# Constant tables copied by ScalarE, batch norm in three chunks, deeper fetch in the second convolution, and another order table for the main stage

## The chip, the cores and the metric

The kernel runs on one core of one Trainium2 chip. The metric is device microseconds (us) from the start to the end of one execution. The core has TensorE (PE in the profile), VectorE (DVE), ScalarE (ACT), GpSimd (POOL) and SyncE (SP). Each works off its own list of instructions in order; an instruction that must wait for another engine waits on a semaphore, and what stands behind it in the same list waits too. In this kernel all DMA transfers are issued by SP.

## The reference, cut to what matters

Input x is 128 images of 128 channels and 16 by 16 places, f32. Two layers are applied.

```
# layer 0
h   = act_quant(bn(groupnorm(x)))                 # 4-bit activations
out = conv3x3(h, weight_quant(w1) * pat1)         # 5 of 9 taps
out = conv3x3(act_quant(bn(out)), weight_quant(w2) * pat2) + groupnorm(x)
x   = x + out
# layer 1, on tokens t = x as [128, 256, 128]
t = t + mamba(ln(t), fwd) + reversed(mamba(ln(reversed t), bwd))
      # in_proj; causal conv of 4 taps; silu; dt = softplus(.); A = -exp(A_log)
      # chunks of 64: exp(segsum(dt*A)) * (C B^T) applied to x*dt, plus carried states
      # y * silu(z), RMS norm, out_proj
t = t + moe(ln(t))        # router over 8 experts, softmax, top 2, expert matrices
```

## The kernel before, in words

**Stages.** The program is one long function, `tile_conv_attn_hybrid_kernel`. (1) A setup stage builds constants, loads x in 64 tiles `xr[i]` of two images each (128 channels by 512 values, 256 KB), quantises the first convolution's weights and computes group norm and batch norm statistics. (2) `conv1` runs over 64 pairs of images: quantise (L525, L527, L192), 5 matmuls (L218), statistics (L542). (3) `conv2` does the second convolution over the same 64 pairs, reads back the first's output from DRAM for all but the first 8 pairs (`fetch`, L615), transposes the result to tokens (L631) and stores it. (4) The main stage runs layer 1 over the 64 pairs. The first three stages are ordered by a scheduler; the main stage stands exactly in the order in which a loop at its end calls its parts.

**Setup.** Two constant tables, `rows0` and `cols0`, hold patterns for later matmuls. POOL fills them in `patterns()` (L376) from `heads` and `triple`, which POOL makes with 18 select instructions (L101, L105). They are stored to DRAM by two DMAs (L489, L490), which stand in SP's list behind the loads of x (L371), the 53 small weight loads of `load_weights` (L278 to L307) and the load of the second convolution's weights (L401). Group norm statistics are taken in four chunks of 48, 48, 24 and 8 images (`cuts`, L414). Per chunk: DVE takes `bn_stats` of each image, except every fourth one, which ACT sums with two passes (L441, L457); DVE combines them in small steps on 128xn tiles (L453 to L468); PE averages over groups with the matrix `grp` (L472, L478); ACT takes a square root (L481); `normed` (L420 to L434) makes a reciprocal with one Newton step and the scales. After the fourth chunk DVE forms the batch norm's scale `sc1` and shift `bi1` (L495 to L511), which every first step of `conv1` needs. The tiles of `conv1` are allocated in memory that the setup stage's tiles leave.

**Main stage.** Each pair goes through parts, each a generator whose steps are placed one by one: `a` layer norm and transposes, `c` time steps and decay (once for two pairs), `x` and `z` projections with the 4-tap convolution on DVE (L895), `xt`, `g`, `s`, `b`, `m` the chunk matrices, `y` their product with x, then gating on POOL (L1028) and squares on ACT; `n` adds the squares on POOL (L1037); `r` sums them on PE (L1045), transposes and takes a power on POOL (L1060); `o` is the output projection (L1072, L1082); `e` the second layer norm and the router, 31 steps, of which 13 in a row are small DVE steps that each read the one before (L1122 to L1145), one power on POOL (L1147), and more small steps; `p` multiplies the tokens by each expert's gate on POOL (L1177); `f` the expert matmuls (L1189). PSUM banks are few: two for x, z and s, two for y and f, four for the rest.

**Order.** `T` (L1200) gives each step a place; a period of 375 places covers two pairs, and the even and the odd pair have places of their own. L1276 adds 375 for each further two pairs, sorts all steps and calls them in that order. So at any place of the list, parts of about ten different pairs are interleaved.

**Keep apart.** Two small helpers bind DVE and POOL: `alone` (L575) remembers the latest small DVE instruction, and `large` (L578) makes the next large POOL instruction (L1028, L1037, L1177) wait for it. Which DVE step a POOL product waits for thus follows from the order in `T`.

Of the kernel before, what the change touches and what calls it, by code (L numbers as in the profile page):

```python
# [14 lines left out]
P = 128  # L15
NT = 256
# [18 lines left out]
def kernel(ctx: ExitStack, tc: tile.TileContext, a: dict):  # L35
# [60 lines left out]
    nc.gpsimd.memset(heads, 0.0)  # L96
    nc.gpsimd.memset(triple, 0.0)
    for m in range(2):
        for q in range(3):
            for t in (3 + 4 * q, 15 + 4 * q):  # L100
                nc.gpsimd.affine_select(  # L101
                    out=heads, in_=heads, pattern=[[-1, NH]], compare_op=ALU.not_equal,
                    fill=-1.0, base=-(64 + 32 * m + t), channel_multiplier=1,
                )
            nc.gpsimd.affine_select(  # L105
                out=triple[:, m : m + 1], in_=triple[:, m : m + 1], pattern=[[0, 1]], compare_op=ALU.not_equal,
                fill=1.0, base=-(64 + 32 * m + q), channel_multiplier=1,
            )
# [114 lines left out]
    def by_weights(how, phase, taps):  # L223

        some = nc.values_load(how[0:1, 0:1], min_val=0, max_val=2)
        with tc.If(some > 0) as cmp:
            with tc.If(some > 1) as cmp2:
                phase(range(9), 3)
            with cmp2.Else():
                phase(range(9), 1)  # L230
        with cmp.Else():
            phase(taps, 1)
# [111 lines left out]
    with tc.tile_pool(name="w1p", bufs=1) as w1p:  # L344

        grp = w1p.tile([P, P], F32, name="grp")
        nc.gpsimd.affine_select(
            out=grp, in_=ones, pattern=[[-4, 32], [0, 4]], compare_op=ALU.is_ge, fill=0.0,
            base=0, channel_multiplier=1,
        )  # L350
        nc.gpsimd.affine_select(
            out=grp, in_=grp, pattern=[[4, 32], [0, 4]], compare_op=ALU.is_ge, fill=0.0,
            base=3, channel_multiplier=-1,
        )
        nc.vector.tensor_scalar(grp, grp, 0.25, None, ALU.mult)
# [4 lines left out]
        with tc.tile_pool(name="setup1", bufs=1) as setup, tc.tile_pool(  # L360
            name="psa", bufs=1, space=PSUM
        ) as psa:
            w1 = w1p.tile([P, 9, P], F32, name="w1", tag="w")
            nc.sync.dma_start(w1, a["L0_conv_w1"])
            weights = conv_weights(wq1, how1, w1p, psa, w1, pat1, CROSS, "c1")
            for _ in range(3):
                next(weights)


            for i in range(NP):  # L370
                nc.sync.dma_start(xr[i], x_c[:, 2 * i : 2 * i + 2, :])  # L371
            rows0 = setup.tile([P, NH, 2, 2, P], BF16, name="rows0")
            cols0 = setup.tile([P, 2, 2, 2, 2, P], BF16, name="cols0")
            far = setup.tile([HD, 1], BF16, name="far")

            def patterns():  # L376
                nc.gpsimd.memset(far, -1e30)
                for h in range(NH):
                    nc.gpsimd.tensor_copy(
                        rows0[:, h].rearrange("p d t l -> p (d t l)"), heads[:, h : h + 1].to_broadcast([P, 4 * P])  # L380
                    )
                    nc.gpsimd.tensor_copy(
                        rows0[0:HD, h].rearrange("p d t (f l) -> p (d t f) l", l=HD),
                        ident[0:HD, 0:HD].unsqueeze(1).to_broadcast([HD, 2 * 2 * 2, HD]),
                    )
                for m in range(2):
                    for d in range(2):
                        sign = 1 - 2 * d
                        nc.gpsimd.tensor_copy(
                            cols0[:, m, d].rearrange("p j f l -> p (j f l)"), triple[:, m : m + 1].to_broadcast([P, 4 * P])  # L390
                        )
                        for half in range(2):
                            nc.gpsimd.affine_select(
                                out=cols0[0:HD, m, d, :, half, :], in_=far.unsqueeze(2).to_broadcast([HD, 2, P]),
                                pattern=[[0, 2], [sign, P]], compare_op=ALU.is_ge, fill=0.0,
                                base=-sign * HD * half - 1, channel_multiplier=-sign,
                            )

            load_weights()
            w2 = w1p.tile([P, 9, P], F32, name="w2", tag="w")  # L400
            nc.sync.dma_start(w2, a["L0_conv_w2"])  # L401

# [11 lines left out]
            cuts = [0, 3 * B // 8, 3 * B // 4, B - max(B // 16, 1), B]  # L414

            def by_scalar(b):

                return b % 4 == 3 and b < cuts[3]

            def normed(c):  # L420

                of = slice(cuts[c], cuts[c + 1])
                var_, gm_, dev_, ga_, qv_, dm_ = (t[:, of] for t in (var, gm, dev, ga, qv, dm))
                nc.vector.reciprocal(ga_, ga_)
                nc.vector.tensor_tensor(dm_, ga_, ga_, ALU.mult)
                nc.vector.tensor_tensor(dm_, dm_, qv_, ALU.mult)
                nc.vector.tensor_scalar(dm_, dm_, -0.5, 1.5, ALU.mult, ALU.add)
                nc.vector.tensor_tensor(ga_, ga_, dm_, ALU.mult)
                nc.vector.scalar_tensor_tensor(shift[:, of], gm_, -1.0, ga_, ALU.mult, ALU.mult)
                nc.gpsimd.tensor_scalar(ares[:, of], ga_, 1.0, SCALE, ALU.add, ALU.mult)  # L430
                nc.gpsimd.tensor_scalar(bres[:, of], shift[:, of], SCALE, None, ALU.mult)
                nc.vector.tensor_tensor(dev_, dev_, ga_, ALU.mult)
                nc.vector.tensor_tensor(var_, var_, ga_, ALU.mult)
                nc.vector.tensor_tensor(var_, var_, ga_, ALU.mult)  # L434

            for c in range(4):
                of = slice(cuts[c], cuts[c + 1])
                for b in range(B)[of]:
                    x_b = xr[b // 2][:, b % 2, :]
                    if by_scalar(b):  # L440
                        nc.scalar.activation(junk, x_b, AF.Copy, accum_out=bst[:, b, 1:2])  # L441
                    else:
                        behind = nc.vector.bn_stats(bst[:, b, :], x_b)
                if c > 0:

                    with tc.issue_after(behind.ins):
# [3 lines left out]
                if mine:  # L450

                    picked = slice(mine[0], cuts[c + 1], 4)
                    nc.vector.tensor_scalar(neg[:, picked], bst[:, picked, 1], -1.0 / NT, None, ALU.mult)  # L453
                    nc.vector.tensor_scalar(bst[:, picked, 1], neg[:, picked], -1.0, None, ALU.mult)
                    nc.vector.tensor_scalar(bst[:, picked, 4], neg[:, picked], -1.0, None, ALU.mult)
# [6 lines left out]
                nc.vector.tensor_tensor(mean_, bst[:, of, 1], bst[:, of, 4], ALU.add)  # L462
                nc.vector.tensor_scalar(mean_, mean_, 0.5, None, ALU.mult)
                nc.vector.tensor_tensor(dm_, bst[:, of, 1], bst[:, of, 4], ALU.subtract)
                nc.vector.tensor_tensor(dm_, dm_, dm_, ALU.mult)
                nc.vector.tensor_tensor(var_, bst[:, of, 2], bst[:, of, 5], ALU.add)
                nc.vector.tensor_scalar(dm_, dm_, 0.25, None, ALU.mult)
                nc.vector.scalar_tensor_tensor(var_, var_, 1.0 / NT, dm_, ALU.mult, ALU.add)  # L468
# [4 lines left out]
                nc.vector.tensor_copy(gm_, gm_ps)  # L473
                nc.vector.tensor_tensor(dev_, mean_, gm_, ALU.subtract)
                nc.vector.tensor_tensor(qv_, dev_, dev_, ALU.mult)
                nc.vector.tensor_tensor(qv_, qv_, var_, ALU.add)
# [3 lines left out]
                nc.vector.tensor_scalar(qv_, gv_ps, EPS, None, ALU.add)  # L480
                nc.scalar.activation(ga_, qv_, AF.Sqrt)  # L481
# [3 lines left out]
                if c == 1:  # L485
                    for _ in weights:
                        pass
                    patterns()
                    nc.sync.dma_start(rows_d, rows0)  # L489
                    nc.sync.dma_start(cols_d, cols0)  # L490
                if c == 3:
# [79 lines left out]
        by_weights(how1, conv1, CROSS)  # L571
# [33 lines left out]
    def conv2(taps, nq):  # L605
        with tc.tile_pool(name="pc", bufs=6) as pc, tc.tile_pool(
# [8 lines left out]
            def fetch(i):  # L615
                if NP > i and i not in kept:
                    qs[i] = pc.tile([P, 2, NT], F32, name=f"q2_{i}", tag="q")
# [31 lines left out]
            for i in range(5):  # L649
# [3 lines left out]
            for i in range(NP):  # L653
                b = 2 * i
                fetch(i + 5)
# [24 lines left out]
    by_weights(how2, conv2, DIAGONAL)  # L680
# [499 lines left out]
    def part_f(i):  # L1180
# [7 lines left out]
        for e in range(NE):  # L1188
# [10 lines left out]
    PERIOD = 375  # L1199
    T = {  # L1200
        ('a',): [[60, 68, 103, 165, 270, 336], [191, 257, 313, 327, 385, 395]],
        ('c',): [
            [420, 423, 452, 460, 468, 479, 483, 502, 515, 520, 522, 523, 526, 534, 537, 543, 548, 549, 581,
             602, 627, 630, 658, 669, 672, 676, 719, 727, 747, 823, 824, 862, 936],
        ],
        ('x', 0, 0): [[598, 604, 609, 613, 622], [783, 784, 790, 791, 805]],
        ('x', 0, 2): [[624, 631, 638, 640, 644], [809, 816, 830, 833, 834]],
        ('x', 0, 1): [[657, 662, 673, 689, 691], [849, 857, 867, 873, 875]],
        ('x', 1, 2): [[681, 684, 701, 703, 712], [866, 879, 881, 891, 896]],
        ('x', 1, 0): [[704, 705, 728, 733, 734], [894, 902, 922, 925, 927]],  # L1210
# [101 lines left out]
```

## Time and profile before

| | |
|---|---|
| runs, median (lowest to highest) | 2554.55 us (2553.18 to 2557.51) |
| the profiled execution's own time | 2554.94 us |
| its span, first to last instruction | 2553.1 us |
| setup, to the first quantising step of conv1 | 0 to 85.7 us |
| conv1 | 85.7 to 173 us |
| conv2 | 173 to 292.3 us |
| main stage, to the first pair's result (L1192 at 438.0) | 292.3 to 438 us |
| main stage, the rest | 438 to 2553.1 us |

Busy shares over the span: PE 95%, DVE 88%, ACT 85%, POOL 64%. The span stands 1.8 us below its execution's time, and that execution 0.4 us above the median. An idle engine costs nothing unless another waits for it; a wait shows as idle time in front of an instruction with the name of what ended it.

### The profile page before, as it was taken

Reading aid. Unit: us, or ns where it says so; the run is one execution under the profiler, and the core shown is the slowest. Engines: PE = TensorE matmul, PEld = TensorE weight load, DVE = VectorE, ACT = ScalarE, POOL = GpSimd, SP = SyncE. Lnnn points to the kernel's source line nnn. Section 1 sums busy time; section 2 is a strip of 40 time slices with the busy share of each in tenths; the row PEclk is TensorE's granted clock in tenths of the full one; section 3 lists DMA queues with packets and bytes.
Section 4 is the critical chain, followed back from the end, with each engine's and each line's share of the span. In section 5 each row is a group of like instructions: output and inputs, shape, how many; then the busy total and the mean of one; then the engine's idle time right before and its main releaser. Section 6 shows DMA issues by size and latency. Waiting matters only on the chain.

```text
span 2553.1 us, 49290 instructions
## 1 busy us (share of the span) xinstructions
PE 2415.3 (95%) x15940; PEld 1479.9 (58%) x15940; DVE 2253.2 (88%) x6163; ACT 2173.0 (85%) x4455; POOL 1629.3 (64%) x1694
## 2 busy tenths in 40 slices
PE   0688889999999999999999999999999999999997
PEld 0235456666666666666666666666666666666663
DVE  8787699999999999999999999999999999999883
ACT  5678699888889998889898888998988899898881
POOL 3468026676666666666666666666667666666666
PEclk9999899999999999999999999999999999999998
DMA  9358633434444444444444344444433443443343
GB/s 287 124 192 281 227 67 110 125 111 123 130 124 122 122 125 118 120 132 128 120 126 124 114 119 129 128 121 119 129 118 117 132 132 121 123 123 116 107 125 107
DMA packets 302167, 339.58 MB, mean 133 GB/s; under 512 B 56768, under 2 KB 226752, under 8 KB 301888
## 3 DMA queue, kind: packets, MB, share of 16 engines
q1 hardware_dynamic: 301888, 336.21, 43.3%
q8 instruction: 133, 2.18, 0.3%
q14 instruction: 146, 1.20, 0.2%
HBM read 262.72 MB, written 56.62 MB: 125 GB/s over the span
## 4 chain that ended last, share of the span: by engine, by line
PE 88%; DMA 4%; DVE 3%; ACT 2%; issue 1%; SPq 1%; POOL 1%; POOLq 0%; ACTq 0%; DVEq 0%
PE f_ps L1189 17%; PE x_ps L877 13%; PE y_ps L1012 10%; PE z_ps L920 9%; PE o_ps L1072 9%; PE sg L965 5%; PE xt_ps L932 4%; PE y_ps L1018 4%; PE g_ps L951 4%; PE cv L218 4%; DMA xr<-in_x 2%; PE n_ps L1045 1%; PE u_ps L1094 1%; PE f_ps L1184 1%; PE u_ps L750 1%
## 5 line engine op out<-in xcount | busy, mean ns | idle before, releaser
L1177 POOL TENSOR_TENSOR gb<-gb,u2T 128x512 f32<-128x512 f32 x512 | 641.3, 1277 | 122.7 <-PE y_ps L1018 68.8
L895 DVE SCALAR_TENSOR_TENSOR xc<-x_ps,cw,xc 128x510 f32<-128x510 f32 (+2 forms) x768 | 571.7, 744 | 46.5 <-ACT xc L889 36.9
L1028 POOL TENSOR_TENSOR yg<-yg,z 128x512 f32<-128x512 f32 x256 | 325.9, 1279 | 352.1 <-DVE yg L1024 155.1
L1189 PE MATMUL f_ps<-gb,ew 128*128 128x512 f32 x1024 | 510.1, 602 | 6.7 <-POOL gb L1177 6.4
L877 PE MATMUL x_ps<-uT,wx 128*128 128x512 f32 x768 | 402.9, 607 | 7.6 <-ACT e L731 3.3
L731 ACT ACTIVATE e<-sg 128x512 f32<-128x512 f32 x512 | 299.3, 591 | 49.9 <-PE sg L965 44.4
L731 ACT ACTIVATE e<-e,ends 128x128 f32<-128x128 f32 x1024 | 325.0, 392 | 0.0
L1012 PE MATMUL y_ps<-e,xt 128*64 128x256 f32 x2048 | 317.8, 389 | 0.2 <-DVE yg L1024 0.2
L993 DVE TENSOR_TENSOR e<-e,g_ps 128x1024 f32<-128x1024 f32 x256 | 311.6, 1217 | 5.5 <-ACT e L731 2.4
L895 DVE SCALAR_TENSOR_TENSOR bc<-x_ps,cw,bc 128x510 f32<-128x510 f32 (+2 forms) x384 | 286.7, 747 | 20.5 <-ACT bc L889 4.1
L1189 PEld LDWEIGHTS f_ps<-gb,ew 128*128 128x128 f32 x1024 | 180.5, 192 | 174.2 <-issue 136.2
L920 PE MATMUL z_ps<-uT,wz 128*128 128x512 f32 x512 | 271.2, 611 | 1.5 <-ACT xc L889 1.0
L889 ACT ACTIVATE xc<-x_ps,cb,cw 128x512 f32<-128x512 f32 x256 | 199.0, 777 | 64.0 <-PE x_ps L877 57.4
L1072 PE MATMUL o_ps<-wo,yg 128*128 128x128 f32 x2048 | 251.4, 276 | 0.2 <-DVE e L998 0.2
L1072 PEld LDWEIGHTS o_ps<-wo,yg 128*128 128x128 f32 x2048 | 240.5, 193 | 11.1 <-DVE g L1149 8.4
L1024 DVE SCALAR_TENSOR_TENSOR yg<-xc,dcol,y_ps 128x512 f32<-128x512 f32 x256 | 189.8, 742 | 50.1 <-PE y_ps L1018 46.8
L1060 POOL TENSOR_TENSOR rr<-rr,mhalf 128x8 f32<-128x8 f32 x64 | 109.9, 1718 | 161.7 <-DVE g L1151 82.7
L1018 PE MATMUL y_ps<-e,xt 128*64 128x128 f32 x2048 | 199.0, 273 | 0.0
L965 PE MATMUL sg<-rows,cols 128*128 128x256 bf16 x1024 | 192.1, 274 | 5.8 <-ACT e L731 2.8
L1018 PEld LDWEIGHTS y_ps<-e,xt 128*64 128x64 f32 x2048 | 147.0, 137 | 74.1 <-DVE e L998 0.5
L218 PE MATMUL cv<-hpad,wq 128*128 128x512 bf16 x640 | 161.7, 396 | 19.5 <-DVE hpad L192 19.4
L1012 PEld LDWEIGHTS y_ps<-e,xt 128*64 128x64 f32 x2048 | 118.9, 136 | 100.9 <-issue 53.8
(256 smaller groups left out, 4813.9 us busy)
## 6 DMA issues: line engine op xcount, KB each, us to landing
gb<-gd SPq DMA_DIRECT2D x256, 512.0 KB
e<-cum SPq DMA_DIRECT2D x256, 256.0 KB
xr<-in_x SPq DMA_DIRECT2D x64, 256.0 KB
cc<-bc SPq DMA_DIRECT2D x128, 128.0 KB
out<-ob SPq DMA_DIRECT2D x64, 256.0 KB
y<-yt SPq DMA_DIRECT2D x60, 256.0 KB
yt<-y SPq DMA_DIRECT2D x60, 256.0 KB
o<-o SPq DMA_DIRECT2D x56, 256.0 KB
```

Of the source, the lines that this page charges most:

```text
L731: nc.scalar.activation(out, in_, func, **more)
L877: nc.tensor.matmul(ps, wx[d][:, n * P : (n + 1) * P], uTs[i], start=True, stop=True)
L895: nc.vector.scalar_tensor_tensor(acc[:, :, to], raw[:, :, of], cw[:, d, n, 3 - back : 4 - back], acc[:, :, to], ALU.mult, ALU.add,)
L920: nc.tensor.matmul(ps, wz[:, d, n * P : (n + 1) * P], uTs[i], start=True, stop=True)
L965: nc.tensor.matmul(sg[:, :, of], c_[:, k, d, s, half, :], r_[:, :, d, s, of], start=True, stop=True)
L993: nc.vector.tensor_tensor(e0.rearrange("p h t l -> p h (t l)"), e0.rearrange("p h t l -> p h (t l)"), gps[i, d, k][:, 0:NT].unsqueeze(1).t ...
L1012: nc.tensor.matmul(y_ps[64 * q : 64 * q + 64, k, :], xt[:, 2 * k + s0, 64 * h : 64 * h + 64], e0[:, h].rearrange("p t l -> p (t l)"), star ...
L1018: nc.tensor.matmul(y_ps[64 * q : 64 * q + 64, k, s1 * P : (s1 + 1) * P], xt[:, 2 * k + s1, 64 * h : 64 * h + 64], e1[:, h, :], start=False ...
L1028: large(nc.gpsimd.tensor_tensor(yg, yg, zs[i, d][:, n, :], ALU.mult))
L1072: nc.tensor.matmul(o_ps[:, (2 * j + d) * P : (2 * j + d + 1) * P], ygs[i, d, n][:, t * P : (t + 1) * P], wo[d][:, n, :], start=(n == 0), s ...
L1177: large(nc.gpsimd.tensor_tensor(gb[:, e], gb[:, e], u2Ts[i], ALU.mult))
L1189: nc.tensor.matmul(f_ps, ew[:, e, :], gbs[i, e], start=False, stop=(e == NE - 1))
```

## The change

Setup: `heads` and `triple` are now made by three DVE reductions of the identity. The tables are filled by ACT in `patterns()`, three large copies ahead of the first tanh and eight small ones behind it, from `far`, which POOL makes. Their stores stand directly behind the loads of x in SP's list; the second convolution's weights and `load_weights` follow them. Statistics are taken in three chunks of 48, 48 and 32 images; ACT's every fourth image ends at image 95. The small steps of the first two chunks are POOL's, two PSUM reads of theirs are ACT's, and their reciprocals are DVE's, placed late (at image 90 and at image 126); the last chunk's small steps are all DVE's. `grp` is scaled by POOL. The branch value of the first convolution is read earlier. conv2: `fetch` runs 8 pairs ahead with 10 buffers, where it ran 5 ahead with 6. Main stage: `T` is replaced. It now has one place list per part, in units of a pair, the same for even and odd pairs (only `c` stays once for two pairs). No part's code is changed.

```
     heads = const.tile([P, NH], F32, name="heads")
     triple = const.tile([P, 2], F32, name="triple")
-    nc.gpsimd.memset(heads, 0.0)
-    nc.gpsimd.memset(triple, 0.0)
...
+    strips = ident[:, HD:].rearrange("p (m r) -> p m r", r=32)
+    nc.vector.tensor_reduce(heads, strips[:, :, 3:27].rearrange("p m (u h) -> p h m u", h=NH), AX.XY, ALU.add)
+    nc.vector.tensor_scalar(heads, heads, -1.0, None, ALU.mult)
+    nc.vector.tensor_reduce(triple, strips[:, :, 0:3], AX.X, ALU.add)
...
+            tables = patterns()
+            made = next(tables)
             w1 = w1p.tile([P, 9, P], F32, name="w1", tag="w")
             nc.sync.dma_start(w1, a["L0_conv_w1"])
             weights = conv_weights(wq1, how1, w1p, psa, w1, pat1, CROSS, "c1")
-            for _ in range(3):
+            with tc.issue_after(made.ins):
                 next(weights)
+            for _ in range(2):
+                next(weights)
+            next(tables)
             for i in range(NP):
                 nc.sync.dma_start(xr[i], x_c[:, 2 * i : 2 * i + 2, :])
...
-            load_weights()
+            nc.sync.dma_start(rows_d, rows0)
+            nc.sync.dma_start(cols_d, cols0)
             w2 = w1p.tile([P, 9, P], F32, name="w2", tag="w")
             nc.sync.dma_start(w2, a["L0_conv_w2"])
+            load_weights()
...
-            cuts = [0, 3 * B // 8, 3 * B // 4, B - max(B // 16, 1), B]
+            cuts = [0, 3 * B // 8, 3 * B // 4, B]
...
-                return b % 4 == 3 and b < cuts[3]
+                return b % 4 == 3 and b < cuts[2]
...
-            for c in range(4):
+            for c in range(3):
                 of = slice(cuts[c], cuts[c + 1])
+                eng = nc.vector if c == 2 else nc.gpsimd
...
+                    if b in (cuts[1] + 42, B - 2):
+                        with tc.issue_after(last.ins):
+                            nc.vector.reciprocal(ga[:, cuts[c - 1] : cuts[c]], ga[:, cuts[c - 1] : cuts[c]])
+                        normed(c - 1)
...
-            for i in range(5):
+            for i in range(8):
                 fetch(i)
...
-                fetch(i + 5)
+                fetch(i + 8)
...
-        ('n', 0): [[1016], [1245]],
-        ('n', 1): [[1065], [1251]],
-        ('r',): [[1068, 1071, 1084, 1091, 1093], [1258, 1268, 1275, 1285, 1291]],
...
-        ('e',): [
-            [1125, 1126, 1144, 1148, 1151, 1168, 1169, 1178, 1188, 1194, 1195, 1197, 1211, 1213, 1220, 1230,
-             1231, 1234, 1246, 1261, 1262, 1278, 1281, 1282, 1286, 1288, 1292, 1294, 1295, 1303, 1308],
-            [1322, 1335, 1346, 1351, 1367, 1371, 1375, 1383, 1392, 1399, 1405, 1406, 1409, 1414, 1415, 1417,
-             1424, 1427, 1433, 1435, 1436, 1450, 1465, 1467, 1472, 1475, 1476, 1479, 1482, 1487, 1514],
-        ],
...
+        ("y", 1, 0): [5.5392, 5.6393, 5.7070, 5.7253],
+        ("y", 1, 1): [5.4582, 5.5056, 5.6802, 5.6946],
+        ("n", 0): [5.6836],
+        ("n", 1): [5.7576],
+        ("r",): [5.80, 5.83, 5.86, 5.89, 5.9300],
...
+        ("e",): [
+            6.1379, 6.1409, 6.2680, 6.3102, 6.3288, 6.3656, 6.38, 6.395, 6.4080, 6.4799, 6.4921, 6.5123, 6.5380, 6.5682,
+            6.5731, 6.5923, 6.5964, 6.6070, 6.6367, 6.6469, 6.6474, 6.7184, 6.7451, 6.7762, 6.7961, 6.7963,
+            6.8026, 6.8275, 6.8646, 6.9316, 7.0848,
         ],
...
+        ("p", 2): [7.3558, 7.7135, 7.9506],
...
-            steps += [(i // 2 * PERIOD + t, len(steps) + n, stream) for n, t in enumerate(places[i % 2])]
+            steps += [(i + t, len(steps) + n, stream) for n, t in enumerate(times)]
```

## The prediction

> **What bounds the kernel now.** I read the busy table by stage first, then the groups of one window, then the timeline around the waits. The table by stage (columns: window and its length, then busy us and instructions of PE, weight loads, DVE, ACT and POOL, granted clock, DMA share, GB/s):
>
> ```profile
> 0.00:85.70 85.70, 6.13 (x23) 4.61 (x24) 65.20 (x224) 40.67 (x130) 23.66 (x86) 1.00 0.80 240
> 173.00:292.30 119.30, 107.52 (x586) 61.20 (x585) 82.40 (x175) 91.92 (x154) 71.28 (x120) 0.97 0.76 256
> 600.00:2400.00 1800.00, 1800.00 (x12297) 1129.89 (x12296) 1650.74 (x4605) 1616.02 (x3331) 1210.81 (x1152) 1.00 0.41 123
> ```
>
> In the main stage PE is busy for all of 1800 us, DVE for 92%, ACT for 90%. How long a pair takes is read from the expert matmuls, 16 records to a pair, in the groups of the same window:
>
> ```profile
> L1189 PE MATMUL f_ps<-gb,ew 128*128 128x512 f32 x838 | 413.8, 596 | 0.0
> ```
>
> 838 / 16 = 52.4 pairs in 1800 us: 34.36 us a pair. The last column is idle time before these matmuls: none. So the main stage, 2553.1 - 292.3 = 2260.8 us or 65.8 such pairs with its ramp and drain, runs at PE's own pace. That pace can only be lost there, hardly won.
>
> How near the other engines are to making PE wait, the timeline shows for POOL and PE around one reduction of the squares:
>
> ```profile
> 1040.17 1.27 POOL L1037 TENSOR_TENSOR sq<-sq,sq 128x512 f32<-128x512 f32 x1 [0.29 <-DVE e L1145]
> 1041.39 1.28 POOL L1177 TENSOR_TENSOR gb<-gb,u2T 128x512 f32<-128x512 f32 x1
> 1042.62 1.05 POOL L1147 TENSOR_TENSOR e<-euler,e 128x4 f32<-128x4 f32 x1
> ...
> 1042.38 0.64 PE L1045 MATMUL n_ps<-sq,chosen 128*32 128x128 f32 x16
> ```
>
> The second add of the squares (L1037) waited for a router step of DVE (L1145), ended at 1041.44, and PE read it at 1042.38: 0.94 us to spare. The router's power (L1147) came after it in POOL's list.
>
> In the setup stage the last wait is this one:
>
> ```profile
> 77.33 0.29 DVE L511 TENSOR_SCALAR bi<-bi,b 128x128 f32<-128x128 f32 x1
> ...
> 79.74 0.43 SPq L489 DMA_DIRECT2D rows_d<-rows  x1
> ...
> 85.72 0.60 ACT L525 ACTIVATE q<-xr,bi,sc 128x256 f32<-128x256 f32 x1 [13.64 <-DMA rows_d<-rows]
> ```
>
> Scale and shift are ready at 77.6, but conv1's first tile lies where the tables lay and waits for their store, issued at 79.7 behind all weight loads.
>
> [...] the next activation starts 1.29 us after the load (1019.37 to 1020.66), so I take 1.28. [...] DVE's 128x128 scaling of the group matrix took 7.84 us while POOL filled tables, against 0.29 us for such a step later. [...]
>
> **The change, part by part.**
>
> *Setup.* Tables: ACT's three copies of 2048 columns have no row; from 1.06 us for 1024 and 0.58 for 512 columns, 0.94 ns a column, an estimate of 2.0 us each. They fit before the tanh, which waited for its weights until 8.68 anyway; without that cover they would cost 6 us. The eight small copies (0.35, 2.8 us in all) push ACT's first sum from 10.2 to about 12.7, and it has caught up soon: a sum takes 0.54 and data for one come every 1.5. The stores move to 51.5 in SP's list and land by about 58. The weight loads behind them end near 81 as now; the first output store behind those is due 16 us into conv1, so nothing waits. The branch read costs nothing: the value is there at 50.
>
> What is late next is the statistics. Tiles of x arrive every 0.75 us from 10.2, the last at 10.2 + 62 x 0.75 = 56.7, and no statistics can end before. ACT has 24 first sums instead of 30. Chunk 1: its sums end near 49.5, POOL's first three steps 0.9, twelve squares at 0.63 and a wait for the group mean of 0.9 bring 59.1; POOL's four steps at 0.35 (its 128x48 steps stand at 0.25 to 0.61), matmul 0.66, root 0.25: 61.4. There the late reciprocal (0.45) holds DVE's list, with one bn_stats (0.33) behind it: 62.2. From there the present last chunk took 77.62 - 68.95 = 8.7 us; 0.5 less, since no other chunk is interleaved: 70.4. Gain 85.7 - 70.4 = **15.3 us**. Bounds: 20 if only the data set it; 8 if every POOL step takes the 0.61.
>
> *conv2.* PE idles 119.3 - 107.5 = 11.8 us, and ACT waited 13.7 us in 16 waits for fetched tiles, 4 to 5 us each on the chain. Three pairs more ahead are 3 x 1.55 = 4.65 us. Gain **8 us** (0 to 11.8: the stage would need 285 GB/s against 256 now and 349 while x is loaded).
>
> *Main stage.* The same instructions, in another order. What counts is where the router of one pair stands to the squares of the next. In the order before, the router's power (places 1278 and 1450) comes after the next pair's second add (1251, and 1065 + 375 = 1440) and after PE's n_ps. In the new table it stands at 6.7184, ahead of that add at 6.7576 and of n_ps at 6.80. So the whole router of a pair (layer norm, transposes, 13 dependent DVE steps, the power) and, by the keep-apart rule, the DVE step after the power must be through before PE may sum the next pair's squares, and that sum starts the next pair's router. This is a loop, closed once a pair.
>
> I walked it along the new lists, from n_ps to the next n_ps, each link either an instruction that it waits for or the one before it in its engine's list, with start-to-start times of the rows now (us):
>
> - PE n_ps and the x matmul behind it 1.4; ACT bc 0.8; DVE two taps, a reciprocal and the mean (L1056) 2.2; POOL power (L1060) 1.7.
> - DVE eight output sums at 0.25, two taps, two small steps 4.0; POOL gate product 1.4.
> - PE two f and two x at 0.86, transposes 0.4, s 0.2, two y groups 2.7, r_ps 0.9, with waits: 7.8.
> - ACT copy 0.2, table load 1.3, silu of bc 1.0, u2T 0.5, xc 0.7, z 0.5, router copy 0.3: 4.4.
> - PE router transpose, two z, one y group 3.4; ACT z, square, bc 1.9.
> - DVE three taps 2.1, yg 0.65, eight router steps 1.55, casts 0.5: 4.8.
> - POOL yg, add, yg, gate product at 1.23 and the power 1.09: 6.0; DVE 0.2; POOL second add 1.4.
>
> PE 12.6, ACT 7.1, DVE 11.2, POOL 10.5: **41.3 us**. For the next pair, which has no time-step part in the way, the same walk gives 40.2. Row sums are a little short: PE's own work by the same rows is 33.1 a pair against 34.36 measured, 4%, which on 12.6 adds 0.5. Mean 40.75 + 0.5 = 41.3 us against 34.36. PE would be busy some 83%. Scaled over the stage: 2260.8 x 41.3 / 34.36 = 2717.5, **+456.7 us**. Bounds: 39 a pair, if hand-offs are shorter than in the rows (+305); 43.5, if waits cost another 0.1 at each of some twenty hand-offs (+601).
>
> Sum: 2553.1 - 15.3 - 8 + 456.7 = 2986.5 of span, and 1.8 around it: **2988 us**. The profiled execution stands 0.4 above the median of the runs, which I leave.
>
> **Rivals.** *PE stays the bound (faster).* The engines run far ahead of PE in the list, and the slack on links that I counted as tight absorbs the loop. It decides at a loop of 34.36 us: below it nothing is lost, and 2553.1 - 23.3 + 1.8 = 2532 results. For it: DVE and ACT have 8 to 10% spare and POOL a third. Against it: 0.94 us to spare now, and the new list puts 1.05 + 0.2 + 1.23 of work into that gap. *Only that edge counts.* The power, the DVE step and a gate product, 2.5 us, less 0.94: 1.5 us a pair, 65.8 x 1.5 = 99, so 2631 us. Against it: a wait of PE delays the work that feeds the same loop. *The change of setup does not do what it says*, since another buffer's release takes the place of the store: 15 us more, inside the range.
>
> **How the numbers follow.** Loop sets the pace 0.84, edge alone 0.07, PE stays the bound 0.07, no difference 0.02. The loop's own bounds, 2837 to 3133, hold about 19 in 20 of its case; 2830 to 3130 thus holds 0.8. Within 0.2% (5 us), which is what a measurement of this kernel can tell from no change, only a chance balance of setup and main stage would fall. Faster 0.07, slower 0.91.
>
> **What the changed kernel's profile would show.** Conv1's first q at about 70, released by DVE's shift and no longer by the table store; few waits for fetched tiles in conv2; then PE at about 83% in the middle with idle time before n_ps released by POOL's add (L1051 there), some 5 us a pair, and smaller ones before the router's matmuls released by ACT. DVE and ACT busy shares fall by the same sixth. If PE is 100% busy in the middle, the loop is wrong. If n_ps doesn't wait but another matmul does, the loop runs elsewhere and only its length is tested. The number fails if hand-offs in the loop overlap more than start-to-start times say.

## The result, and the profile after

The changed kernel takes 3177.81 us (median; 3171.98 to 3180.04) against 2555.43 us (2553.18 to 2557.51) for the kernel before: a ratio of 1.2432, 95% interval 1.2411 to 1.2454. Forecast was 2988 us with a range up to 3130. The direction was right, the loss is 622 us instead of 433, and the time lies above the range. The profiled execution has a span of 3170.2 us.

The table by stage of the changed kernel (columns: window and its length, then busy us and instructions of PE, weight loads, DVE, ACT and POOL, granted clock, DMA share, GB/s); the windows are the setup, conv2 and the middle of the main stage:

```profile
0.00:72.50 72.50, 5.07 (x19) 3.60 (x20) 53.61 (x164) 42.62 (x121) 27.07 (x94) 1.00 0.88 276
162.80:276.20 113.40, 106.35 (x586) 62.05 (x587) 83.00 (x175) 91.25 (x154) 71.11 (x118) 0.97 0.79 269
700.00:2800.00 2100.00, 1798.88 (x11090) 1050.59 (x11090) 1577.07 (x4161) 1453.82 (x3004) 1091.53 (x1039) 0.92 0.32 95
```

The first two stages became shorter: conv1's first tile starts at 72.5 instead of 85.7 us, the main stage at 276.2 instead of 292.3. The third line has the loss. PE is busy for 1798.88 of 2100 us, 86%, where it was 100%. The third column from the end has what the forecast did not have: the granted clock, the share of its full clock that PE is given, is 0.92 on average, where it was 1.00.

The groups of PE in that window, the expert matmuls, the x projection and the sum of squares:

```profile
L1203 PE MATMUL f_ps<-gb,ew 128*128 128x512 f32 x755 | 428.4, 662 | 8.5 <-POOL gb L1191 8.5
L891 PE MATMUL x_ps<-uT,wx 128*128 128x512 f32 x568 | 369.2, 737 | 0.0
L1059 PE MATMUL n_ps<-sq,chosen 128*32 128x128 f32 x760 | 51.5, 354 | 251.2 <-POOL sq L1051 250.8
```

755 / 16 = 47.2 pairs in 2100 us: 44.5 us a pair. Idle time before the sum of squares is 250.8 / 47.2 = 5.3 us a pair, as forecast ("some 5 us"). But the matmuls themselves are slower too: 662 ns for an expert matmul where the kernel before has 596, and 737 for the x projection, where the group of before, from 600 to 2400 us, reads

```profile
L877 PE MATMUL x_ps<-uT,wx 128*128 128x512 f32 x628 | 323.8, 597 | 0.0
```

So a pair is 6.4 us of idle PE and 38.1 us of busy PE; the forecast had 6.9 and 34.4. The place where this happens shows in two timelines of the changed kernel. POOL's list, released by the router's last step before the power (DVE L1159), runs through six instructions to the second add of the squares:

```profile
1494.50 1.26 POOL L1042 TENSOR_TENSOR yg<-yg,z 128x512 f32<-128x512 f32 x1 [2.59 <-DVE e L1159]
1495.73 1.28 POOL L1051 TENSOR_TENSOR sq<-sq,sq 128x512 f32<-128x512 f32 x1
1496.96 1.27 POOL L1042 TENSOR_TENSOR yg<-yg,z 128x512 f32<-128x512 f32 x1
1498.19 1.27 POOL L1191 TENSOR_TENSOR gb<-gb,u2T 128x512 f32<-128x512 f32 x1
1499.42 1.04 POOL L1161 TENSOR_TENSOR e<-euler,e 128x4 f32<-128x4 f32 x1
1500.80 1.49 POOL L1051 TENSOR_TENSOR sq<-sq,sq 128x512 f32<-128x512 f32 x1 [0.35 <-DVE g L1163]
```

PE in the same stretch:

```profile
1497.06 0.43 PE L1059 MATMUL n_ps<-sq,chosen 128*32 128x128 f32 x8
1502.35 0.66 PE L1059 MATMUL n_ps<-sq,chosen 128*32 128x128 f32 x8 [4.87 <-POOL sq L1051]
1502.94 2.08 PE L891 MATMUL x_ps<-uT,wx 128*128 128x512 f32 x2
```

The same two x matmuls take 1.02 us elsewhere in the pair. The granted clock in the same place, in stretches of 3 us (again the third column from the end):

```profile
1497.00:1500.00 3.00, 0.46 (x9) 0.16 (x8) 2.51 (x4) 1.91 (x5) 3.00 (x4) 1.00 0.00 0
1500.00:1503.00 3.00, 0.65 (x9) 0.27 (x9) 2.12 (x7) 1.02 (x4) 1.95 (x2) 0.59 0.00 0
1503.00:1506.00 3.00, 3.00 (x7) 1.29 (x6) 0.14 (x1) 0.95 (x3) 0.00 (x0) 0.50 0.00 0
1506.00:1509.00 3.00, 3.00 (x13) 1.75 (x12) 2.16 (x6) 2.78 (x7) 0.36 (x1) 0.77 0.00 0
```

PE waits from 1497.5 to 1502.3; its clock falls to half at 1500.5 and is back at 1507.4. About 1.8 us of this hit an idle PE, 5 us hit matmuls. Those stand in the loop: the chain that ended last, as the profile follows it back, runs through them,

```profile
1500.80 1.50 POOL sq L1051
1502.31 0.04 issue
1502.35 0.66 PE n_ps L1059 x8
1503.01 2.01 PE x_ps L891 x2
1505.02 0.43 PE sg L979 x2
1505.44 1.71 PE f_ps L1203 x2
```

and on through PE, ACT and POOL to the next pair's second add.

### The profile page after: what moved, and what is told of

Same layout as the page of the kernel before. It is cut to its first block, busy times and chain, and to the rows that moved or that the text cites. A ratio compares the mean times of both kernels' runs of the same rounds, so it can differ in the third digit from the quotient of the medians.

```text
span 3170.2 us, 49096 instructions
## 1 busy us (share of the span) xinstructions
PE 2645.5 (83%) x15936; PEld 1522.5 (48%) x15936; DVE 2353.5 (74%) x6103; ACT 2170.5 (68%) x4445; POOL 1631.4 (51%) x1702
## 4 chain that ended last, share of the span: by engine, by line
PE 47%; POOL 24%; ACT 14%; issue 7%; DMA 4%; DVE 3%; SPq 0%; POOLq 0%; DVEq 0%; ACTq 0%
PE x_ps L891 10%; POOL gb L1191 8%; PE f_ps L1203 8%; PE o_ps L1086 7%; POOL sq L1051 5%; POOL yg L1042 5%; PE z_ps L934 3%; PE y_ps L1026 3%; PE cv L209 3%; ACT L745 3%; PE sg L979 2%; ACT bc L745 2%; POOL e L1161 2%; PE g_ps L965 2%; POOL rstda L609 2%
## 5 line engine op out<-in xcount | busy, mean ns | idle before, releaser
L1191 POOL TENSOR_TENSOR gb<-gb,u2T 128x512 f32<-128x512 f32 x512 | 645.1, 1273 | 264.2 <-issue 98.7
L1042 POOL TENSOR_TENSOR yg<-yg,z 128x512 f32<-128x512 f32 x256 | 323.3, 1272 | 538.7 <-DVE rstda L606 413.5
L1203 PE MATMUL f_ps<-gb,ew 128*128 128x512 f32 x1024 | 580.7, 663 | 16.9 <-POOL gb L1191 16.3
L891 PE MATMUL x_ps<-uT,wx 128*128 128x512 f32 x768 | 502.1, 741 | 9.6 <-ACT e L745 5.3
L1059 PE MATMUL n_ps<-sq,chosen 128*32 128x128 f32 x1024 | 69.0, 352 | 333.8 <-POOL sq L1051 333.2
L1203 PEld LDWEIGHTS f_ps<-gb,ew 128*128 128x128 f32 x1024 | 189.9, 208 | 165.0 <-issue 105.4
L903 ACT ACTIVATE bc<-x_ps,cb,cw 128x512 f32<-128x512 f32 x128 | 99.2, 775 | 242.1 <-PE x_ps L891 242.1
L1045 ACT ACTIVATE sq<-yg 128x512 f32<-128x512 f32 x256 | 161.2, 630 | 136.8 <-POOL yg L1042 134.3
L891 PEld LDWEIGHTS x_ps<-uT,wx 128*128 128x128 f32 x768 | 158.0, 231 | 177.2 <-issue 75.7
L1012 DVE TENSOR_TENSOR e<-e,g_ps 128x512 f32<-128x512 f32 x256 | 174.2, 680 | 56.3 <-ACT e L745 56.2
L979 PE MATMUL sg<-rows,cols 128*128 128x256 bf16 x1024 | 212.0, 291 | 1.3 <-DVE bc L909 1.2
```

Source lines behind the costliest of these rows:

```text
L891: nc.tensor.matmul(ps, wx[d][:, n * P : (n + 1) * P], uTs[i], start=True, stop=True)
L903: nc.scalar.activation(acc, raw, AF.Identity, bias=cb[:, d, n : n + 1], scale=cw[:, d, n, 3:4])
L979: nc.tensor.matmul(sg[:, :, of], c_[:, k, d, s, half, :], r_[:, :, d, s, of], start=True, stop=True)
L1042: large(nc.gpsimd.tensor_tensor(yg, yg, zs[i, d][:, n, :], ALU.mult))
L1191: large(nc.gpsimd.tensor_tensor(gb[:, e], gb[:, e], u2Ts[i], ALU.mult))
L1203: nc.tensor.matmul(f_ps, ew[:, e, :], gbs[i, e], start=False, stop=(e == NE - 1))
```

## The experiments

Pair times below are worked out as above, from the count of expert matmuls between 700 and 2400 us, divided by 16; as that window holds some 40 pairs, they are good to about 0.2 us. The clock is the mean over the whole span unless a window is named. A time that stands without a ratio is that of one run; four runs of one kernel lay within 0.3% of each other.

**Where the loss sits: the place table put back, and the place table alone.** First the changed kernel with the table and loop of before:

```
-        ("n", 1): [5.7576],
+        ('n', 1): [[1065], [1251]],
...
-            steps += [(i + t, len(steps) + n, stream) for n, t in enumerate(times)]
+            steps += [(i // 2 * PERIOD + t, len(steps) + n, stream) for n, t in enumerate(places[i % 2])]
```

> The changed kernel with the main stage's place table and its loop put back as before; setup and conv2 stay changed. Theory: all of the loss comes from the table, and the two earlier stages keep what the changed kernel's profile shows, 292.35 - 276.2 = 16.2 us at the start of the main stage: 2555.4 - 16.2 = 2539 us, main stage again 2261 us with PE at full clock. Rival: the earlier stages gain nothing in the end, because the main stage's first loads come too early for what they need: 2555 us. Rival: part of the loss comes from the changed setup (DRAM tables, buffers, POOL's load), and the main stage stays longer than 2261 us: over 2560.

Measured: 2542.14 us, ratio 0.9944 (0.9927 to 0.9961), 34.5 us a pair, no wait of PE in the middle. This version is the fastest here, if only by 0.6%. The 13 us are less than the 16.2 that the changed kernel's profile had promised, and the profile says where: here conv2 ended at 280.8 and not at 276.6 us, though the program is the same up to there. Second, the kernel before with the changed table, the reverse of that diff.

> The kernel before with only the main stage's place table and loop of the changed kernel. Theory: the table alone makes the loss: main stage 2894 us as in the changed kernel, 292.3 + 2894 + 1.8 = 3188 us, 44.5 us a pair, PE waits some 5 us a pair for the second add of the squares, clock about 0.92. Rival: setup's changes share in it: clearly under 3150.

Measured: 3191.23 us, 44.5 us a pair, clock 0.923. The table alone makes the whole loss.

**Does the wait cost more than its own length?** 24 spare matmuls, whose result nothing reads, put in front of the sum:

```
         n_ps = bank(f"n_ps{i}", "o")
+        for _ in range(24):
+            nc.tensor.matmul(n_ps[:, 2 * P : 3 * P], ident, ew[:, 0, :], start=True, stop=True)
         for d in range(2):
```

> The changed kernel with 24 spare matmuls of 128x128 f32 ahead of each pair's sum of squares, into columns of its PSUM bank that nothing reads; 24 x 0.11 = 2.6 us of PE time a pair, put where PE would wait some 5 us. Theory (the wait itself lowers PE's clock to half for about 7 us, and the work after it, which stands in the loop, takes about 2.5 to 3.5 us longer): the wait left is about 2.3 us, the clock stays at 1.0, the two matmuls behind the sum go back from 2.08 to about 1.03 us, and a pair takes 41 to 42 us instead of 44.5: 2950 to 3015 us, although PE has more to do. Rival (the clock is low for another reason, or what it slows is not in the loop): no change, 3178 us, or up to 24 x 0.11 x 64 = 169 us more, 3347.

Measured: 3060.08 us, ratio 1.1968 (1.1948 to 1.1988) to the kernel before. PE has more to do and the kernel is 118 us faster. Its groups of PE between 700 and 2400 us:

```profile
L1205 PE MATMUL f_ps<-gb,ew 128*128 128x512 f32 x639 | 326.4, 602 | 7.4 <-POOL gb L1193 7.4
L891 PE MATMUL x_ps<-uT,wx 128*128 128x512 f32 x480 | 257.7, 619 | 17.8 <-ACT e L745 17.8
L1058 PE MATMUL n_ps<-ew,ident 128*128 128x128 f32 x1920 | 220.9, 275 | 0.0
L1061 PE MATMUL n_ps<-sq,chosen 128*32 128x128 f32 x640 | 29.9, 282 | 6.4 <-POOL sq L1051 6.4
```

The x projection is back at 619 ns, the clock at 1.00 in this window, 42.6 us a pair. I had mis-sized the edit: each of the 24 f32 matmuls of the program is two instructions here (1920 records in 40 pairs, 48 a pair), so the spare work took 5.5 us and filled the whole wait; only 6.4 us of waiting are left in 40 pairs. The time is above what I expected (2950 to 3015). The spare work can itself have delayed a sum, so 42.6 us is an upper bound of the loop at full clock and the gain a lower bound of what the clock cost. The trace shows that the bound is close: in every second pair PE still waited some 0.3 us for the second add, and in the others the spare matmuls ended less than 0.1 us after that add. The other bound follows from the changed kernel: its 39 stretches of half clock each held 5.5 us of matmuls on average, which at full clock would take 2.8 us less, so the loop at full clock is not under 44.5 - 2.8 = 41.7 us (an estimate from these figures).

The same with 12 spare matmuls:

> The changed kernel with 12 spare matmuls of 128x128 f32 ahead of each pair's sum of squares instead of 24; 24 of them took 5.52 us and filled the whole wait. Theory ([...] loop itself 42.5 us): 2.76 us of spare work, a wait of about 2.5 to 3 us left, clock 0.98 to 1.0, 42.5 us a pair, 3060 us as with 24. Rival (24 stood in the loop's way and cost part of their gain): 41.3 us a pair as the prediction's walk gave, about 2985 us. Rival (any wait lowers the clock in proportion): clock about 0.96, 3110 to 3130 us.

Measured: 3107.8 us, 43.3 us a pair, clock 0.963. The third reading, or near it: 2.8 us of spare work were in, the waits left were 2.2 to 3.0 us, and the clock still fell behind most of them (30 stretches of half clock after 40 waits). So waits of 3.0 us and less were followed by it too; the last section has the counts.

**Is it the router's power, ahead of the add, that closes the loop?** The power and what follows it were moved behind the next pair's sum:

```
-            6.5731, 6.5923, 6.5964, 6.6070, 6.6367, 6.6469, 6.6474, 6.7184, 6.7451, 6.7762, 6.7961, 6.7963,
-            6.8026, 6.8275, 6.8646, 6.9316, 7.0848,
+            6.5731, 6.5923, 6.5964, 6.6070, 6.6367, 6.6469, 6.6474, 6.8134, 6.8401, 6.8712, 6.8911, 6.8913,
+            6.8976, 6.9225, 6.9300, 6.9350, 7.0848,
```

> The changed kernel with the router's power and the steps behind it (places 6.7184 to 6.9316) moved behind the next pair's second add and sum of squares (6.8134 to 6.9350). Theory of the prediction (the power ahead of the add is the link that closes the loop too late): the power, the step after it and their hand-offs, 1.0 + 0.2 + 0.35 = 1.5 us, leave the loop, and with a shorter wait the clock recovers part: 3178 - 65 x 1.5 = 3080 us or less. Rival (the loop is closed by the keep-apart wait of the gating product L1042 on the router's last step, with the four large POOL products behind it; the power is only one piece of that list): the power goes but others take its place, 0.3 us a pair: 3140 to 3178 us.

Measured: 3120.09 us, 43.4 us a pair, clock 0.942: between the two. The wait for the add fell to 149.3 us in 60 waits, but a new one of 35.5 us stands before the gates' transpose (it waits for DVE L1173, 0.9 us a pair). How much of the 58 us was clock, the same edit with the 12 spare matmuls tells:

> The same 12 spare matmuls together with the late router power, so that what the power's place does to the loop is seen without the clock's part (late power alone: 3120 us at a clock of 0.94, 43.4 us a pair). Theory of the prediction (the power ahead of the add lengthens the loop by 1.5 us): 42.5 - 1.5 = 41.0 us a pair, 3060 - 96 = 2964 us. Rival (without the power other links take its place, PE now waits 0.9 us a pair for the gates' transpose): 42.2 us or more, 3040 to 3060 us; then the 58 us of late power alone were the shorter wait's clock.

Measured: 3042.24 us, 42.1 us a pair, clock 0.985. Against the 42.6 us of the loop at full clock the power's place is worth some 0.5 us a pair, not 1.5, the new wait included; five stretches of half clock were left in 40 pairs, which can hide 0.2 us more. The forecast's edge is not what closes the loop; most of what its removal won was clock.

**The keep-apart waits.** All of them taken out of the changed kernel (no data passes through them):

```
     def large(made):
-        if latest:
+        if False:
```

> The changed kernel without the keep-apart waits of POOL's large products on DVE's small steps (no data passes through them). Theory (they tie the gating products and the adds to the router of the pair before, and with that close the loop): the loop opens in part; of the 5 us wait for the second add half or more goes, the clock rises to 0.98 or more, 37 to 38.5 us a pair: 2690 to 2800 us. If they alone closed it: 34.4 us, 2540 us. Rival (the loop runs through data and the lists alone): 44 us, 3150 us or more. Rival (DVE and POOL hinder each other without them, and what is won is lost to longer steps): POOL's large products over 1.5 us, 2850 us or more.

Measured: 2817.37 us, a little above the 2800 of the first reading; 38.3 us a pair, clock 1.00 in the middle. The waits of PE between 700 and 2400 us (us in total, times, longest):

```profile
PE n_ps L1059 <- POOL sq L1051: 77.0, 45, 1.7
PE rt_ps L1122 <- ACT rts L1120: 28.0, 44, 0.9
PE x_ps L891 <- ACT e L745: 18.6, 42, 0.4
```

This is the largest single piece of the loop that an experiment took out: 4.3 of the 8.2 us that a pair lost at full clock (42.6 - 34.4). The rest, 3.9 us, is left when data and the order of the lists alone bind the engines; part of it may be DVE steps that take longer without these waits, as the run on the old order below shows them to do. Which of the products count, the next run was to tell: the gating products L1042 and the adds L1051 freed, the gates' products L1191 still bound, with 12 spare matmuls.

```
-        large(nc.gpsimd.tensor_tensor(yg, yg, zs[i, d][:, n, :], ALU.mult))
+        nc.gpsimd.tensor_tensor(yg, yg, zs[i, d][:, n, :], ALU.mult)
...
-        large(nc.gpsimd.tensor_tensor(sq, sq, sqs[i, d, 1], ALU.add))
+        nc.gpsimd.tensor_tensor(sq, sq, sqs[i, d, 1], ALU.add)
```

> The changed kernel without the keep-apart waits of the gating products and the adds of squares; the products by the experts' gates keep theirs; 12 spare matmuls ahead of each pair's sum keep the clock up. Without any keep-apart wait the pair took 38.3 us, with all of them 42.5 at full clock. If the gating products and the adds are what closes the loop: 38.3 us, 2820 us. If every large product's wait lengthens it: half of the 4.2 us, 40.4 us, 2930 us. If the gates' products are what counts: 42 us or more, 3040 us.

Measured: 2994.64 us, 41.5 us a pair, clock 0.981: only 1.1 of the 4.3 us. The gates' product, which stands between the gating product and the power in POOL's list, took the wait over: between 700 and 2400 us it waited 220.6 us for a router step of DVE, where it waited 27.7 us for it in the changed kernel. That is what the helper does: `large` hands each DVE step's wait to the next product that asks for one and then forgets it, so a product that no longer asks leaves its wait to the next. This run therefore doesn't part the three kinds of products; it shows that freeing some of a row is worth little while another in the same list is bound.

What these waits are for showed in the old order, where the same edit was made to the 2542 us version:

> The changed setup and fetch with the old place table (2542 us) and without any keep-apart wait. If the waits cost nothing where PE is the bound: 2542 us within 3. If they do what their name says, and without them DVE's and POOL's steps take longer: POOL's large products over 1.3 us or DVE's small steps longer, PE waits, over 2550 us. If they cost PE something in the ramp: 2535 to 2540 us.

Measured: 2620.13 us, ratio 1.0255 (1.0233 to 1.0276): the second reading, with DVE's steps longer and POOL's not (1.28 us as before). One router step of DVE between 700 and 2400 us, first with the waits:

```profile
L1143 DVE TENSOR_TENSOR sel<-lg,mx 128x32 f32<-128x32 f32 x100 | 19.1, 191 | 1.7
```

and without them:

```profile
L1143 DVE TENSOR_TENSOR sel<-lg,mx 128x32 f32<-128x32 f32 x94 | 56.2, 597 | 1.6
```

The timeline of the version without them has such a step whole; it starts inside a POOL product and ends with it:

```profile
1506.48 1.28 POOL L1191 TENSOR_TENSOR gb<-gb,u2T 128x512 f32<-128x512 f32 x1
1506.67 1.13 DVE L1143 TENSOR_TENSOR sel<-lg,mx 128x32 f32<-128x32 f32 x1
```

The step took 1.13 us, where its mean with the waits is 0.19, and ended 0.04 us behind the product. The waits are worth 78 us in the old order, where PE is the bound, and cost some 4 us a pair in the new one.

**Is it a loop, or one late product?** The sum of squares was placed 0.06 of a pair later, so that PE has other matmuls to do:

```
-        ("r",): [5.80, 5.83, 5.86, 5.89, 5.9300],
+        ("r",): [5.86, 5.88, 5.90, 5.91, 5.9300],
```

> The changed kernel with the sum of squares of each pair placed 0.06 of a pair later (places 5.80 to 5.89 of part r become 5.86 to 5.91), so that PE has other matmuls (x, sg, f) to do while the second add is not ready. If only this one product is late and there is no loop: PE is busy again all the time, 34.4 us a pair, 2545 us. Loop theory: the wait is cut into smaller ones that come back elsewhere (ahead of x, sg and the router's matmuls); [...] the clock stays near 1.0, and the pair takes 39.5 to 41.5 us: 2830 to 2960 us. If the sum's new place lengthens the loop as much as it fills: 42.5 us and more, 3060 us.

Measured: 2988.14 us, 41.5 us a pair, clock 0.959. PE's waits:

```profile
PE x_ps L891 <- ACT e L745: 55.7, 41, 1.6
PE x_ps L891 <- DVE xc L909: 38.3, 41, 0.9
PE sg L979 <- ACT e L745: 34.4, 41, 1.3
PE rt_ps L1122 <- ACT rts L1120: 25.8, 41, 0.9
```

The wait for the add is gone altogether, and PE waits elsewhere. This is a loop, and its length sets the pace. That the clock would stay near 1.0 was wrong: it fell behind two waits of 0.94 and 1.30 us, or of 1.30 and 1.56 us, within 5 us as well, and the time came out 28 us above the expectation's end.

**Setup and conv2.** The deeper fetch alone, on the kernel before:

```
-                    qs[i] = pc.tile([P, 2, NT], F32, name=f"q2_{i}", tag="q")
+                    qs[i] = pc.tile([P, 2, NT], F32, name=f"q2_{i}", tag="q", bufs=10)
...
-            for i in range(5):
+            for i in range(8):
                 fetch(i)
...
-                fetch(i + 5)
+                fetch(i + 8)
```

> The kernel before with conv2's fetch 8 pairs ahead and 10 buffers, nothing else. Theory of the prediction: conv2 8 us shorter: 2547 us. By the changed kernel's profile (conv2 from its first step to the main stage 113.4 us against 118.9): 5.5 us shorter, 2550 us. Rival (the fetches wait for the DMA rate, not for their issue): 2555 us, waits for fetched tiles as many as before.

Measured: 2555.02 us, ratio 0.9999 (0.9991 to 1.0008), as in the rival's reading. ACT still waits 9.8 us for fetched tiles (13.7 before), and the stage moves 257 GB/s, where it moved 256. The changed setup alone (old table, fetch 5 ahead):

> The kernel before with the changed setup alone (place table and fetch depth as before). The deeper fetch alone gave a ratio of 0.9999, both together 0.9944. If the setup carries all of it: conv1 starts at 72.5 instead of 85.7 us, takes 2.6 us longer, and the time is 2555 - 11 to 13 = 2542 to 2545 us. If the deeper fetch is needed to carry the gain on through conv2: 2548 to 2552 us. The prediction's own step: 15.3 us, 2540 us.

Measured: 2544.73 us, ratio 0.9953 (0.9935 to 0.9971). All of the gain that can be told from nothing is the setup's.

## Why the prediction was wrong in its size

**The loss and its mechanism: right.** PE is no longer the bound, the wait stands before the sum of squares and is released by POOL's second add, 5.3 us a pair; smaller waits stand before the router's matmuls, released by ACT; PE is busy 86% of the middle where 83% was forecast, in part because the same matmuls took longer. The rivals "PE stays the bound" and "only that edge" fell.

**The size: two terms were short.** The span was forecast as 2986.5 us and is 3170.2: 183.7 more.

| term | forecast | measured | difference |
|---|---|---|---|
| gain of setup to conv2, at the start of the main stage | 23.3 | 16.1 | +7.2 |
| main stage at full clock (from the run with 24 spare matmuls: span 3062.3, main stage from 281.8) | 2717.5 | at most 2780.5 | +63.0 |
| what the lower clock adds (2894.0 - 2780.5) | 0 | at least 113.5 | +113.5 |

The step that failed is "The same instructions, in another order", and with it the walk's rule that PE costs the start-to-start times of the rows now: "PE 12.6" of the 41.3 us. Those rows were taken with PE never idle. The same walk found PE idle for some 7 us a pair, mostly in one piece, and never asked what such a wait does to the matmuls after it. In the changed kernel's trace each wait of 4.5 to 5.0 us (39 of 39) brought 6.8 us at half clock, which began 3 to 4 us into the wait and ran on over the matmuls behind it. The run with 24 spare matmuls shows the price: it left the lists of all other engines as they were, gave PE more to do, and was 118 us faster.

The second term is the loop itself, 41.7 to 42.6 us at full clock against 41.3 (the walk's own parts, 12.6, 7.1, 11.2 and 10.5, add up to 41.4). It lies inside the bounds given (39 to 43.5), a small error for a sum of some fifty links. That the sum came so near doesn't show each link right: the edge that the forecast took for the decisive one was not. The bounds' upper end, +601 us, would have held the loop; nothing in the range stood for the clock.

**Which edge closes the loop: wrong.** The forecast put it on the router's power, which now precedes the add. Moved away, it gave some 0.5 us a pair at full clock. The keep-apart waits, which the forecast named only for the DVE step after the power, are the largest piece found (4.3 us): POOL's list above shows the whole row of products, not the add alone, standing behind the router's last step.

**Setup: nearly right.** Forecast was a first tile at 70.4 us, released by DVE's shift; it is 72.5, so released:

```profile
72.46 3.06 ACT L539 ACTIVATE q<-xr,bi,sc 128x256 f32<-128x256 f32 x6 [5.85 <-DVE bi L525]
```

The late reciprocal with the bn_stats behind it should have ended at 62.2 and ended at 63.0. From there to the shift it took 9.4 us instead of 8.2. My figure came from the last chunk of before, whose steps are on 128x8; the new last chunk's are on 128x32. Most of the excess lies ahead of the step that reads the group variance: 3.6 us from the chunk's first step to there, against 2.7 before, with DVE idle for 1.5 us of it in waits for PE and ACT. Which of the two, the wider tiles or the missing other chunk, makes this was not tried. Then conv1 took 90.3 instead of 87.7 us: POOL's first tiles waited 2.9 and 1.7 us for weight loads, which stand behind the table stores in SP's list (`load_weights` issues 42 loads; the 53 named above is a miscount). Why those tiles wait for these loads was not tried, and stays open.

**conv2: wrong.** "Three pairs more ahead are 3 x 1.55 = 4.65 us" supposed that the fetches come late because they are issued late. With eight ahead and nothing else changed the transfer rate is the same, and the kernel's time is too. In the eleven profiled executions with fetch 8 conv2 took 113.8 to 120.0 us from its first step to its last transposes, 116.9 in the mean; in three with fetch 5 it took 118.8 to 119.3. That is 2 us, and the 5.5 us of the changed kernel's own profile are the shortest of the eleven.

## What to carry to other kernels

When a new order makes the busiest engine wait, the cost is the wait and what follows from it: in this kernel a wait of 4.5 to 5.0 us took half of PE's clock from some 5.5 us of the work after it, and where that work is part of the loop which caused the wait, the loop pays twice. Price those links at half speed, or put cheap independent matmuls into the gap (24 of them made this kernel 118 us faster). And look for a bound instruction anywhere in an in-order list between two points, not only at its end: the edge that the eye fell on was worth 0.5 us a pair, the waits that held the row before it 4.3.

## What the runs showed of the hardware that was not expected

The clock fell behind shorter waits than the 4.5 to 5.0 us of the changed kernel. Counted from the traces of seven runs, over the main stage between 700 and 2400 us (PE's wait for the second add, and whether a stretch of half clock began in it or just behind it):

| wait | waits | followed by half clock |
|---|---|---|
| under 1.5 us | 100 | 1 |
| 1.5 to 2.2 us | 84 | 13 |
| 2.2 to 2.8 us | 22 | 14 |
| 2.8 to 3.0 us | 13 | 10 |
| 3.0 to 3.4 us | 47 | 42 |
| 4.5 to 5.0 us | 39 | 39 |

The stretches in these traces lasted 3.4 or 6.8 us and nothing between; all 39 of the changed kernel lasted 6.8 us. Of the 166 waits of 1.5 to 3.4 us 79 were followed by half clock and 87 were not, so the length of this one wait does not tell which.

Half clock also followed shorter waits that came close together. In the run with the sum placed later no wait was over 1.6 us, and 123 of 1700 us still ran at half clock. Three windows of that run show one such place (PE's busy time is the first number after the length):

```profile
1138.18:1141.59 3.41, 1.36 (x5) 0.52 (x5) 2.52 (x9) 3.41 (x9) 2.77 (x3) 1.00 0.00 0
1141.59:1145.00 3.41, 3.41 (x20) 1.21 (x21) 1.85 (x4) 1.83 (x6) 0.00 (x0) 0.50 0.00 0
1145.00:1148.42 3.42, 3.42 (x32) 3.40 (x33) 2.70 (x8) 1.67 (x4) 2.89 (x2) 1.00 0.02 5
```

In the first PE was idle for 3.41 - 1.36 = 2.05 us, in two waits for ACT, one of 1.27 us that began ahead of the window and one of 1.56 us; the second ran at half clock with PE busy throughout, and the third at full clock again. Whether other work shows the same was not tried.
